# Layer three of a positional-bias network: tiles of four keys by thirty-two sums, or of eight keys by sixteen

## The chip, the cores and the metric

The kernel runs on one core of one Trainium2 chip. Such a core has five engines that each work through a queue of their own, in order: TensorE (matrix products; PE in the profile, PEld its weight loads), VectorE (DVE), ScalarE (ACT), GpSimd (POOL) and SyncE (SP, which here only starts transfers). They wait for one another through semaphores. Transfers are carried by sixteen DMA engines, whoever starts them. The metric is device time in microseconds for one execution; lower is better.

## The reference, cut to what matters

The reference is a transformer block with sampled keys, followed by a second attention layer. The part that the change touches is a small network that gives each pair of query and key an additive bias before the softmax:

```python
pos  = grid_q[:, :, None, :] - grid_kv[:, None, :, :]      # 16 groups, 1024 queries, 64 keys, 2
bias = sign(pos) * log1p(abs(pos))
bias = relu(bias @ cpb_w1 + cpb_b1)                         # 2 -> 128
bias = relu(bias @ cpb_w2 + cpb_b2)                         # 128 -> 128
bias = (bias @ cpb_w3 + cpb_b3)                             # 128 -> 1
sim  = einsum('bhid,bhjd->bhij', qh, kh) + bias
attn = softmax(sim, axis=-1)
```

There are 16 groups (2 images, 8 heads), so the network runs on 16 x 1024 x 64 pairs, all in float32. Its second layer is by far the largest product of the whole program.

## The kernel before

**Slots.** A group's 64 keys are cut into 16 slots of four keys; there are 256 slots, numbered `s` in the main loop (NG x NSL). One transfer for every four slots brings a table `fb` of the positional terms, from which ScalarE makes `ta` and `tb` for sixteen keys (`st_tables`).

**Layer 1** (`st_layer1`, L593) is one VectorE instruction per slot: it adds the two tables with broadcasts, clamps at zero and writes `h1`, 128 channels by 4096 (32 rows, 4 keys, 32 columns). Three buffers of `h1` let it run two slots ahead.

**Layer 2** (`st_layer2`, L610) is TensorE's. The 128 output channels are cut into four blocks `z` of 32. For one block, eight matmuls (two halves `h` of the queries, four keys `q`) write a PSUM tile of 128 partitions by 2 x 512: partition 32q + l holds lane l of key q. Each float32 matmul shows as two instructions in the profile. ScalarE empties the four tiles with bias and relu (L616 for `rx`, L618 for `ua` and `ub`).

**Adding the blocks.** The third layer is a weighted sum over the 128 channels. The size of each weight is applied early: even blocks are multiplied by a ratio of weights when VectorE adds them to their odd neighbour (`st_sum`, L626: `ua` from blocks 0 and 1, `ub` from blocks 2 and 3); only a sign per lane is left for the end. For that, the four channels that share a lane have been put in a fitting order by selections on GpSimd at the start (`swap`, L191 to L211). Then a transfer that adds at its destination, started by GpSimd (L628), puts `ub` onto `ua`. What is left of a slot is one tile `ua` of four keys by 32 sums.

**Layer 3** (`st_layer3`, L649) multiplies `ua` by `w3s`, a matrix of signs, to add the 32 lanes of each key. It runs once for every two slots, three slots after the first of them: four matmuls (two halves `h`, two slots `e`), each 32 output rows by 512. The rows of a group's 16 slots collect in one PSUM tile `sim`, which also takes the product of queries and keys (L640) at the group's end. The last two slots skip the adding transfer and use more matmuls instead.

**Order.** Within an engine, instructions run in the order in which a scheduler places them at build time, mostly that of the program; `tc.issue_after` pins single ones. On VectorE, a slot in the steady state is h of two slots ahead, then `ub` of the slot before, then `ua` of this slot. Background work (attention's sampling for later groups until about 1300 us, softmax steps for finished groups) is put between the slots on all engines. After the loop, at 1990 us, come an output projection (L822), an MLP (L875) and the second attention (L994, L1092), which the change doesn't touch.

Of the kernel before, what the change touches and what calls it, by code (L numbers as in the profile page):

```python
# [10 lines left out]
ALU = mybir.AluOpType  # L11
# [10 lines left out]
KT = 16  # L22
LAST = 2
KS = 6
# [12 lines left out]
    ("bq", 4), ("bv", 4), ("bp", 4), ("dwb", 1), ("cb1", 1), ("cb3", 1),  # L37
    ("w1x", 1), ("w1y", 1), ("cb2", 4), ("w3", 4), ("dww", 36),
]
# [8 lines left out]
@with_exitstack  # L48
def conv_seq_kernel(ctx: ExitStack, tc: tile.TileContext, x, xt, kst, cst, vec, wsm, outw, w1, w2, wl, out):
    nc = tc.nc  # L50


    cp = ctx.enter_context(tc.tile_pool(name="cp", bufs=1))
    kp = cp.tile([P, 384], F32, name="kp")
    vs = cp.tile([P, NV], F32, name="vs")
    nc.scalar.dma_start(out=vs, in_=vec)
    xv = x.rearrange("b (k p) n -> p k b n", p=P)
    ident = kp[:, 0:128]

# [9 lines left out]
    sc = cp.tile([P, 9], F32, name="sc")  # L69
    w3s = cp.tile([P, 60], F32, name="w3s")  # L70
    nc.gpsimd.memset(w3s, 0.0)

# [66 lines left out]
    with tc.tile_pool(name="lp", bufs=2) as lp:  # L139
# [29 lines left out]
        nc.scalar.dma_start(out=cs, in_=cst)  # L169
        nc.scalar.dma_start(out=kp, in_=kst)  # L170

# [17 lines left out]

        def swap(w, of, n):  # L190
            w = w.rearrange("p (z c) -> p z c", z=4)  # L191
            t = ph.tile([P, 10, n], F32, tag="hx" if n > 1 else "swap", name=f"swap{n}")
            g, ne, a1, a3, keep, t0, t1 = t[:, 0:4], t[:, 4], t[:, 5], t[:, 6], t[:, 7], t[:, 8], t[:, 9]
            nc.gpsimd.tensor_scalar(g, w, 0.0, None, ALU.is_ge)
            for o, u, v in ((ne, g[:, 1], g[:, 3]), (a1, g[:, 0], g[:, 1])):
                nc.gpsimd.tensor_tensor(o, u, v, ALU.subtract)
                nc.gpsimd.tensor_tensor(o, o, o, ALU.mult)
            nc.gpsimd.tensor_tensor(a1, a1, ne, ALU.mult)
            nc.gpsimd.tensor_tensor(a3, ne, a1, ALU.subtract)
            nc.gpsimd.tensor_scalar(keep, ne, -1.0, 1.0, ALU.mult, ALU.add)  # L200
            for dst, src in of:
                d, v = (e.rearrange("p (z c) -> p z c", z=4) for e in (dst, src))
                nc.gpsimd.tensor_copy(d[:, 2], v[:, 2])
                nc.gpsimd.tensor_tensor(d[:, 0], v[:, 0], keep, ALU.mult)
                for z, a in ((1, a1), (3, a3)):
                    nc.gpsimd.tensor_tensor(t0, v[:, z], a, ALU.mult)
                    nc.gpsimd.tensor_tensor(d[:, 0], d[:, 0], t0, ALU.add)
                    nc.gpsimd.tensor_scalar(t1, a, -1.0, 1.0, ALU.mult, ALU.add)
                    nc.gpsimd.tensor_tensor(t1, t1, v[:, z], ALU.mult)
                    nc.gpsimd.tensor_tensor(t0, v[:, 0], a, ALU.mult)  # L210
                    nc.gpsimd.tensor_tensor(d[:, z], t0, t1, ALU.add)  # L211

        swap(kp[:, 256:384], [(cw2, kp[:, 128:256])], 32)
        w3 = vs[:, VOFF["w3"] : VOFF["w3"] + 4]
        swap(w3, [(sc[:, 0:4], w3), (sc[:, 4:8], vs[:, VOFF["cb2"] : VOFF["cb2"] + 4])], 1)
        nc.gpsimd.tensor_scalar(sc[:, 8:9], sc[:, 1:2], 0.0, 2.0, ALU.is_ge, ALU.mult)
        nc.gpsimd.tensor_scalar(sc[:, 8:9], sc[:, 8:9], 1.0, None, ALU.subtract)
        nc.gpsimd.tensor_scalar(sc[:, 0:4], sc[:, 0:4], sc[:, 8:9], None, ALU.mult)
        for z in (1, 3):
            nc.gpsimd.tensor_tensor(sc[:, 4 + z : 5 + z], sc[:, 4 + z : 5 + z], sc[:, z : z + 1], ALU.mult)  # L220
        for u in range(4):
            nc.gpsimd.tensor_copy(w3s[32 * u : 32 * u + 32, 28 + u : 29 + u], sc[32 * u : 32 * u + 32, 8:9])
        state = {}
# [153 lines left out]
        def sample(ci):  # L377
# [23 lines left out]
            for i, (b, k) in enumerate(G):  # L401
# [29 lines left out]
                for f in range(2):  # L431
                    r = slice(64 * f, 64 * f + 64)
                    d = kvz[r, f, :].rearrange("p (e i t) -> p e i t", e=2, t=4)
                    v, u = (
                        t[r].rearrange("p (i e t) -> p e i t", e=2, t=4)
                        for t in (ps[:, 0:J], sg[:, 4, f, i * J : (i + 1) * J])
                    )
                    for e in range(2):
                        nc.vector.scalar_tensor_tensor(
                            d[:, e], v[:, e], bns[r, k : k + 1], u[:, e], ALU.mult, ALU.add  # L440
                        )
# [103 lines left out]
        for _ in head:  # L545
            pass
        next(v)
        next(n)
# [5 lines left out]
        NS = NG * NSL  # L554
        tabs, h1s, sums, sims, logits = {}, {}, {}, {}, {}
        evicted, raw = {}, {}
# [46 lines left out]
        def st_layer2(s):  # L603
            h1 = h1s.pop(s)
            r = []
            for z in range(4):
                ps = zp.tile([P, 2, 512], F32, name="ps2")
                for h in range(2):
                    for q in range(4):
                        nc.tensor.matmul(  # L610
                            ps[32 * q : 32 * q + 32, h, :], cw2[:, 32 * z : 32 * z + 32],
                            h1[:, 16 * h : 16 * h + 16, q, :], start=True, stop=True,
                        )
                o = lp.tile([P, 2, 512], F32, name=("rx", "ua", "rx", "ub")[z], bufs=(3, 5, 3, 4)[z])
                if z % 2 == 0:
                    nc.scalar.activation(o, ps, AF.Relu, bias=sc[:, 4 + z : 5 + z])  # L616
                else:
                    nc.scalar.activation(o, ps, AF.Relu, bias=sc[:, 4 + z : 5 + z], scale=sc[:, z : z + 1])  # L618
                r.append(o)
                if z % 2 == 1:  # L620
                    evicted.setdefault(s, []).append(nc.cur_bb.bb.instructions[-1])
            sums[s] = r

        def st_sum(s, z):
            r = [t.rearrange("p h n -> p (h n)") for t in sums[s][z : z + 2]]
            nc.vector.scalar_tensor_tensor(r[1], r[0], sc[:, z : z + 1], r[1], ALU.mult, ALU.add)  # L626
            if z == 2 and s < NS - LAST:
                nc.gpsimd.dma_start(out=sums[s][1], in_=sums[s][3], accum_op=ALU.add)  # L628

        def st_layer3(s):  # L630
            gi, i = divmod(s // 2, NSL // 2)
            b, k, f = groups[gi]
            if i == 0:
                sims[gi] = simp.tile([P, 512], F32, name="sim")
            if i == NSL // 2 - 1:
                assert state[chain_of[b, k][0]] is None
                for h in range(2):
                    for e in range(2):
# [4 lines left out]
                        )  # L643
            parts = (1,) if s < NS - LAST else (1, 3)
            for z in parts:
                for h in range(2):
                    for e in range(2):
                        q = 64 * h + 32 * e
                        nc.tensor.matmul(  # L649
                            sims[gi][q : q + 32, :], w3s[:, 28 - 4 * i : 60 - 4 * i], sums[s + e][z][:, h, :],  # L650
                            start=(i == 0), stop=(i == NSL // 2 - 1 and z == parts[-1]),
                        )
            for e in range(2):
                sums.pop(s + e)

# [62 lines left out]
        for s in range(NS):  # L718
            if s > 0:
                st_sum(s - 1, 2)  # L720
            if s % 4 == 0 and s // 4 + 1 < 4 * NG:
                load_tables(s // 4 + 1)
# [29 lines left out]
            if tail is not None:  # L752
                with tc.issue_after(evicted[s][s % 4 == 0]):
                    tail = tail if next(tail, 0) is None else None
            if s % 2 == 1 and s >= 3:
                st_layer3(s - 3)
                if (s - 2) % NSL == NSL - 1:
                    tail = softmax_steps(s // NSL - 1)
        st_sum(NS - 1, 2)
        st_layer3(NS - 2)  # L760
        tail = softmax_steps(NG - 1)
# [417 lines left out]


def _layout(np, inputs):
    a = {k: np.asarray(v) for k, v in inputs.items()}
# [6 lines left out]
    def twice(v):  # L1189
# [7 lines left out]
        "dwb": twice(L0["off_dw_b"].reshape(DH, 1)), "cb1": L0["cpb_b1"].reshape(P, 1),  # L1197
        "cb2": np.tile(L0["cpb_b2"].reshape(4, 32).T, (4, 1)),
        "w3": np.tile(L0["cpb_w3"].reshape(4, 32).T, (4, 1)),
        "cb3": np.broadcast_to(L0["cpb_b3"].reshape(1, 1), (P, 1)),  # L1200
# [26 lines left out]
    def quarters(w):  # L1227
# [8 lines left out]
        "xt": a["x"].reshape(B, NCH, P, 8, P).transpose(4, 0, 1, 3, 2),  # L1236
        "kst": np.concatenate(
            [np.eye(P, dtype=np.float32), L0["cpb_w2"], np.broadcast_to(L0["cpb_w3"].reshape(1, P), (P, P))],
            axis=1,
        ),  # L1240
        "cst": _constants(np), "vec": vec, "wsm": wsm,
# [25 lines left out]
```

## Time and profile before

| | us |
| --- | --- |
| Median of 3 runs (2735.78 to 2737.64) | 2737.45 |
| Span of the profiled execution | 2735.9 |
| First matmul of layer 2 | 41.70 |
| End of the slot loop (first projection matmul) | 1990.13 |
| Pair of slots in a quiet stretch (1423.88 to 1438.47) | 14.59 |
| h, one per slot on VectorE | 4.40 each |
| A sum of two blocks on VectorE | 1.28 each |
| Issue of an adding transfer on GpSimd | 0.87 each |

A profile page gives for each engine the busy time and its share of the span, then the span in 40 slices with the busy share of each in tenths, then the DMA queues, then the chain of work that ended last, followed back from the end. Under it stand groups of equal instructions: line, engine, operation, tile written and tiles read, shape and count, busy time and mean of one in ns, and behind the second bar how long the engine was idle just before them and what ended it. Lines on transfers give the size of one and the median time from issue to landing. Answers in order of time give start and length in us.

### The profile page before, as it was taken

To read this page: it belongs to the slowest core of one execution; us is meant where nothing else is said; L and a number is where in the kernel's file an instruction comes from. 1 tells how busy PE (TensorE), PEld (TensorE's weight loads), DVE (VectorE), ACT (ScalarE), POOL (GpSimd) and SP (SyncE) were. 2 spreads that over 40 slices of the span, in tenths; PEclk is the share of its full clock that TensorE was granted. 3 is DMA by queue.
4 is the path that set the end of the run, shared out by engine and by line. 5 is a ranking of instruction groups with operands and counts; after the bars stand their busy time and mean duration, and the time that the engine had idled before them with its cause. 6 is when DMAs were issued, how large, how long until landed. Compare 5 with 4: busy or idle time off the path is not lost.

```text
span 2735.9 us, 46606 instructions
## 1 busy us (share of the span) xinstructions
PE 2718.1 (99%) x20114; PEld 983.6 (36%) x20114; DVE 2242.0 (82%) x1331; ACT 1686.5 (62%) x2164; POOL 362.8 (13%) x426
## 2 busy tenths in 40 slices
PE   9999999999999999999999999999999999999999
PEld 3332323232334333334333333333344444446455
DVE  6999999998999899999999999999864574366454
ACT  4786897788878788876876776686722021124040
POOL 3111111111111111111111111111133333000000
PEclk9999999999999999999999999999999999999999
DMA  5444444444444443444444444444331011000000
GB/s 186 92 95 91 92 100 86 87 102 100 86 87 101 101 86 82 98 93 86 86 93 90 86 90 92 86 91 92 74 139 46 32 45 46 16 16 0 31 0 31
DMA packets 64685, 214.32 MB, mean 78 GB/s; under 512 B 11104, under 2 KB 13664, under 8 KB 61792
## 3 DMA queue, kind: packets, MB, share of 16 engines
q0 software_dynamic: 36864, 135.28, 26.7%
q1 hardware_dynamic: 26752, 74.98, 7.8%
q8 instruction: 159, 2.61, 0.4%
q10 hardware_dynamic: 864, 1.07, 0.1%
q14 instruction: 46, 0.38, 0.0%
HBM read 71.59 MB, written 6.55 MB: 29 GB/s over the span
## 4 chain that ended last, share of the span: by engine, by line
PE 92%; DVE 4%; ACT 2%; issue 1%; DMA 1%; SPq 0%; DVEq 0%; ACTq 0%
PE ps L610 59%; PE sw L875 14%; PE sw L994 9%; PE sim L649 4%; PE sw L1092 2%; DVE h L593 2%; PE sw L822 1%; PE psg L499 1%; PE sim L640 0%; DVE ua L626 0%; DVE ub L626 0%; DMA fb<-fdr 0%; PE pkv L425 0%; DVE xs L830 0%; ACT rx L616 0%
## 5 line engine op out<-in xcount | busy, mean ns | idle before, releaser
L610 PE MATMUL ps<-h,cw 128*32 128x512 f32 x16384 | 1791.2, 593 | 7.4 <-ACT rx L616 5.0
L593 DVE CUSTOM_DVE_ANT_1 h<-ta,tb 128x4096 f32<-128x4096 f32 (+1 forms) x257 | 1131.8, 4404 | 85.1 <-PE ps L610 81.5
L610 PEld LDWEIGHTS ps<-h,cw 128*32 128x32 f32 x16384 | 544.1, 110 | 1215.6 <-issue 1160.9
L616 ACT ACTIVATE rx<-ps,sc 128x1024 f32<-128x1024 f32 x512 | 568.4, 1110 | 219.8 <-PE ps L610 216.6
L628 POOL DMA_DIRECT2D ua<-ub x254 | 220.0, 866 | 1697.7 <-DVE ub L626 1609.9
L618 ACT ACTIVATE ua<-ps,sc 128x1024 f32<-128x1024 f32 x256 | 308.0, 1203 | 117.1 <-PE ps L610 116.8
L618 ACT ACTIVATE ub<-ps,sc 128x1024 f32<-128x1024 f32 x256 | 307.6, 1202 | 89.2 <-PE ps L610 88.9
L626 DVE SCALAR_TENSOR_TENSOR ua<-rx,sc,ua 128x1024 f32<-128x1024 f32 x256 | 327.3, 1278 | 32.6 <-ACT ua L618 32.6
L626 DVE SCALAR_TENSOR_TENSOR ub<-rx,sc,ub 128x1024 f32<-128x1024 f32 x256 | 326.8, 1276 | 5.8 <-ACT ub L618 5.6
L875 PE MATMUL sw<-xb,w1t 128*128 128x512 f32 x448 | 193.7, 592 | 1.3 <-DVE xs L121 1.3
L875 PE MATMUL sw<-hm,w2t 128*128 128x512 f32 x448 | 193.6, 592 | 0.0
L121 DVE TENSOR_TENSOR hm<-hm,sw 128x1024 f32<-128x1024 f32 x56 | 67.6, 1220 | 112.5 <-PE sw L875 112.3
L649 PE MATMUL sim<-ua,w3s 128*32 128x512 f32 x1024 | 135.7, 594 | 0.0
L875 PEld LDWEIGHTS sw<-xb,w1t 128*128 128x128 f32 x448 | 85.1, 190 | 108.8 <-issue 105.4
L875 PEld LDWEIGHTS sw<-hm,w2t 128*128 128x128 f32 x448 | 85.2, 190 | 107.1 <-issue 106.1
L884 ACT ACTIVATE hm<-hm,vs 128x512 f32<-128x512 f32 x64 | 42.7, 713 | 129.5 <-DVE hm L121 129.5
L121 DVE TENSOR_TENSOR xs<-xs,sw 128x1024 f32<-128x1024 f32 (+1 forms) x48 | 55.6, 1171 | 74.6 <-PE sw L994 36.0
L574 ACT ACTIVATE ta<-fb,vs 128x512 f32<-128x512 f32 x64 | 88.8, 1388 | 17.7 <-DMA fb<-fdr 17.7
L994 PE MATMUL sw<-aT,vt 128*128 128x512 f32 x224 | 96.7, 593 | 0.3 <-ACT aT L1074 0.3
L909 ACT COPY hm<-sw 128x1024 f32<-128x1024 f32 x8 | 8.1, 1009 | 132.4 <-PE sw L875 132.4
L103 POOL TENSOR_TENSOR w1t<-w1t 128x512 f32<-128x512 f32 x32 | 58.4, 1844 | 112.0 <-DMA w1t<-in_w 111.4
L290 ACT ACTIVATE prod<-qa,vs 128x56 f32<-128x56 f32 (+4 forms) x180 | 64.1, 442 | 0.0
(227 smaller groups left out, 1533.3 us busy)
## 6 DMA issues: line engine op xcount, KB each, us to landing
ua<-ub POOLq DMA_DIRECT2D x254, 512.0 KB, 4.6
fb<-fdr SPq DMA_DIRECT2D x64, 512.0 KB, 4.7
w1t<-in_w SPq DMA_DIRECT2D x8, 1024.0 KB, 4.9
w2t<-in_w SPq DMA_DIRECT2D x8, 1024.0 KB, 4.9
xn<-in_x SPq DMA_DIRECT2D x8, 512.0 KB, 5.1
xnt<-in_xt SPq DMA_DIRECT2D x8, 512.0 KB, 5.7
xs<-in_x SPq DMA_DIRECT2D x16, 256.0 KB, 5.7
out<-xs SPq DMA_DIRECT2D x16, 256.0 KB, 2.1
```

Of the source, the lines that this page charges most:

```text
L121: nc.vector.tensor_tensor(out, a, b_, op)
L290: nc.scalar.activation(dst, src, AF.Copy, scale=col("dww", 12 * m + t))
L574: nc.scalar.activation(ta.rearrange("p j x -> p x j"), fb[:, 0], AF.Identity, bias=col("cb1"), scale=col("w1x"))
L593: nc.vector._custom_dve(TENSOR_ADD_SAT, out=h1[:, y : y + step].rearrange("p y t x -> p (y t x)"), in0=a.unsqueeze(1).to_broadcast([P, ste ...
L610: nc.tensor.matmul(ps[32 * q : 32 * q + 32, h, :], cw2[:, 32 * z : 32 * z + 32], h1[:, 16 * h : 16 * h + 16, q, :], start=True, stop=True,)
L616: nc.scalar.activation(o, ps, AF.Relu, bias=sc[:, 4 + z : 5 + z])
L618: nc.scalar.activation(o, ps, AF.Relu, bias=sc[:, 4 + z : 5 + z], scale=sc[:, z : z + 1])
L626: nc.vector.scalar_tensor_tensor(r[1], r[0], sc[:, z : z + 1], r[1], ALU.mult, ALU.add)
L628: nc.gpsimd.dma_start(out=sums[s][1], in_=sums[s][3], accum_op=ALU.add)
L649: nc.tensor.matmul(sims[gi][q : q + 32, :], w3s[:, 28 - 4 * i : 60 - 4 * i], sums[s + e][z][:, h, :], start=(i == 0), stop=(i == NSL // 2 ...
L875: nc.tensor.matmul(ps[:, m, :], w[:, a, k, m * P : (m + 1) * P], x[:, b_, k, :], start=(k == 0), stop=(k == 1),)
L994: nc.tensor.matmul(ps[:, m, :], w[:, a, k, c + m * P : c + (m + 1) * P], x[b_][:, k, :], start=(k == 0), stop=(k == nk - 1),)
```

## The change

Two tiles of four keys by 32 sums become one of eight keys by 16 sums before layer 3 reads them. Channels are ordered by the sign of their third-layer weight, so that two neighbouring lanes (2l and 2l + 1) may be added before the sign is applied. `st_fold` adds the odd lanes of an even slot's tile onto its even lanes, `st_join` brings the odd lanes of the next slot into the freed odd lanes and adds that slot's even lanes to them. All three act on 64 of 128 partitions, every second one. The aim is to let layer 3 run once for four slots with the four matmuls that it used for two.

```diff
+        def lanes(s, i):
+            return sums[s][1].rearrange("(l e) h n -> l e (h n)", e=2)[:, i]
+        def st_fold(s):
+            with tc.issue_after(added[0]):
+                nc.gpsimd.dma_start(out=lanes(s, 0), in_=lanes(s, 1), accum_op=ALU.add)
+        def st_join(s):
+            nc.sync.dma_start(out=lanes(s, 1), in_=lanes(s + 1, 1))
+            with tc.issue_after(added[0]):
+                nc.gpsimd.dma_start(out=lanes(s, 1), in_=lanes(s + 1, 0), accum_op=ALU.add)
...
         def st_sum(s, z):
-            if z == 2 and s < NS - LAST:
+            if z == 2 and s < NS - 1:
                 nc.gpsimd.dma_start(out=sums[s][1], in_=sums[s][3], accum_op=ALU.add)
+                added[0] = nc.cur_bb.bb.instructions[-1]
...
         def st_layer3(s):
-            gi, i = divmod(s // 2, NSL // 2)
+            gi, i = divmod(s // 4, NSL // 4)
...
         for s in range(NS):
             if s > 0:
                 st_sum(s - 1, 2)
+            if s % 2 == 0 and 2 <= s < NS - 2:
+                st_fold(s - 2)
+            if s % 2 == 1 and 3 <= s < NS - 1:
+                st_join(s - 3)
...
-            if s % 2 == 1 and s >= 3:
-                st_layer3(s - 3)
+            if s % 4 == 2 and s >= 6:
+                st_layer3(s - 6)
```

`added[0]` is the newest adding transfer of a whole slot, so fold and join stand behind the next slot's in GpSimd's queue. The last four slots are not joined; they use other signs (`w3u`) and ten matmuls.

The sums get other buffers, twelve tiles as before:

```diff
-                o = lp.tile([P, 2, 512], F32, name=("rx", "ua", "rx", "ub")[z], bufs=(3, 5, 3, 4)[z])
+                name, bufs = (("rx", 3), (("ua", 4), ("uo", 2))[s % 2], ("rx", 3), ("ub", 3))[z]
+                o = lp.tile([P, 2, 512], F32, name=name, bufs=bufs)
```

At the start, the selections on GpSimd go, and an order of channels is computed instead: a load `pst` (transposed second-layer weights and index tables), two rank matmuls with one column each ahead of the query product, a dozen small operations, and later a matmul with a permutation and sixteen tiny ones, which give layer 2's weights and the scalars in the new order.

```diff
-        swap(kp[:, 256:384], [(cw2, kp[:, 128:256])], 32)
-        w3 = vs[:, VOFF["w3"] : VOFF["w3"] + 4]
-        swap(w3, [(sc[:, 0:4], w3), (sc[:, 4:8], vs[:, VOFF["cb2"] : VOFF["cb2"] + 4])], 1)
+        nc.tensor.matmul(ps[:, 0:1], tri, po_, start=True, stop=True)
+        nc.tensor.matmul(ps[:, 512:513], one, po_, start=True, stop=True)
...
+        def arrange():
+            ps = flat("perm")
+            nc.tensor.matmul(ps[:, 0:P], w2t, perm, start=True, stop=True)
+            for z in range(4):
+                for u in range(4):
+                    nc.tensor.matmul(
+                        ps[32 * u : 32 * u + 32, 512 + 2 * z : 514 + 2 * z], perm[:, 32 * z : 32 * z + 32], wb,
+                        start=True, stop=True,
+                    )
+            nc.scalar.copy(cw2, ps[:, 0:P])
...
         for _ in head:
             pass
+        arrange()
         next(v)
```

## The prediction

> **What bounds the kernel now.** I read the engines' busy times first, then the slices, the chain of waits, the groups, and last the stage in question by stretches and in order of time.
>
> ```profile
> PE 2718.1 (99%) x20114; PEld 983.6 (36%) x20114; DVE 2242.0 (82%) x1331; ACT 1686.5 (62%) x2164; POOL 362.8 (13%) x426
> PE   9999999999999999999999999999999999999999
> DVE  6999999998999899999999999999864574366454
> PE 92%; DVE 4%; ACT 2%; issue 1%; DMA 1%; SPq 0%; DVEq 0%; ACTq 0%
> L610 PE MATMUL ps<-h,cw 128*32 128x512 f32 x16384 | 1791.2, 593 | 7.4 <-ACT rx L616 5.0
> L649 PE MATMUL sim<-ua,w3s 128*32 128x512 f32 x1024 | 135.7, 594 | 0.0
> q0 software_dynamic: 36864, 135.28, 26.7%
> ua<-ub POOLq DMA_DIRECT2D x254, 512.0 KB, 4.6
> out<-xs SPq DMA_DIRECT2D x16, 256.0 KB, 2.1
> ```
>
> TensorE is busy 99% of the span and carries 92% of the chain: removed matmul time is real time unless something else takes over. That something is VectorE: in slices 2 to 28 (the slot loop, 43 to 1990 us) it stands at 9 nearly throughout. Layer 3 (L649) shows 135.7 us, but records overlap their neighbours, so I price it from the order of time, in a stretch without background work:
>
> ```profile
> 1423.88 13.92 PE L610 MATMUL ps<-h,cw 128*32 128x512 f32 x128
> 1430.99 4.42 DVE L593 CUSTOM_DVE_ANT_1 h<-ta,tb 128x4096 f32<-128x4096 f32 x1 [0.91 <-PE ps L610]
> 1436.91 0.87 POOL L628 DMA_DIRECT2D ua<-ub  x1 [6.84 <-DVE ub L626]
> 1437.61 1.04 PE L649 MATMUL sim<-ua,w3s 128*32 128x512 f32 x8
> 1438.47 13.92 PE L610 MATMUL ps<-h,cw 128*32 128x512 f32 x128
> ```
>
> From 1423.88 to 1438.47 two slots take 14.59 us. L610's 128 instructions run from 1423.88 to 1437.61 (13.73 us, 0.107 us each, a slot 6.87); L649's eight take the other 0.86 us, also 0.107 each. VectorE has 0.91 us idle here; back to back its slot is 6.73 us (starts of h at 1002.08, 1008.81, 1015.54). Where attention's other work runs on it as well, it has none:
>
> ```profile
> 1050.00:1100.00 50.00, 50.00 (x470) 15.75 (x466) 49.93 (x36) 42.00 (x63) 6.47 (x7) 1.00 0.39 80
> 1400.00:1450.00 50.00, 50.00 (x472) 15.10 (x464) 45.45 (x21) 34.44 (x32) 5.18 (x6) 1.00 0.47 96
> ```
>
> The columns after the length are PE, PEld, DVE, ACT and POOL busy us, clock, DMA share, GB/s. Both windows have a full TensorE; VectorE has 0.07 us left in one, 4.55 us in the other.
>
> [...] The trace disagrees for the adding transfers: 4.6 us to landing, and 26.7% of 2735.9 us over 254 of them is 2.87 us on the engines. [...] the trace has 2.1 us for out<-xs, to memory. [...] each link added below costs a full landing; before has no such link. [...] the issue of L628 takes 0.85 to 0.91 us beside h (L593), but 1.32 us where the small TENSOR_SCALAR of L383 falls on it. More issues on GpSimd should not slow VectorE.
>
> **The change part by part.**
> Removed: layer 3 runs once for four slots on eight-key tiles, not once for two. In the built order 516 matmuls become 262, so 254 fewer, two instructions each: 508 x 0.107 = **54.4 us** off TensorE, 0.86 per four slots, 1.4 per 50 us of loop.
> What VectorE lets through: its work is unchanged, so in each 50 us window the gain is at most its idle time. From 50 to 1300 us, 15 of 25 windows leave it at least 1.4 us (21 us in all); the other ten, at 48.74 to 50.00 busy, leave 4.0 us together. From 1300 to 1990 us every window has 2.7 us or more idle: 13.8 x 1.4 = 19.4. Sum 44.4; **10 us are lost to VectorE**.
> Added transfers: per pair of slots one fold (64 partitions, 256 KB), one plain copy on SP (256 KB), one join (256 KB): 126 of each. Issue: 252 more on GpSimd at 0.45 to 0.87 us, at most 219 us over 1947 us beside 220 us now; that engine mostly waits (1610 us for ub's sum). Engines: q0 goes from 26.7% to about 40% (252 x 1.44 us more). Neither binds.
> Their latency is the new wait. From the start T of a slot, sum ub ends and L628 issues at T+6.1 (1430.75 to 1436.91 above). The engines have it done at about +9.9 (landing less 0.8 of tail); the fold behind it needs half of 2.87: +11.3, landed +12.1. Copy on SP, 2.4 us[...]: +14.6. The join stands behind the next slot's L628 on GpSimd (issue at +13.0, engines done at +16.8): +1.4 +0.8 = landed **+19.1**. Layer 3 reads it three slots after T: 3 x 6.87 = **+20.6**. So 1.5 us to spare, against 3.0 before (L628 issued at +6.1 landed at +10.7 and was read two slots after T, at +13.7). Behind a late layer 3 stands all of layer 2 in TensorE's queue. A VectorE burst (the TENSOR_REDUCE of L305 is 2.98 us) puts the chain up to 1.5 us late if it falls in the half of the slots that feed a join: about one such per window in the 15 windows with room, 0.7 us each: **-10 us**. From 1300 us on, bursts are 1.3 us and fit.
> Bounds of the chain: if stride-2 halves take the engines the full 2.87 us and the copy 5.7 us (the slowest 256 KB load), landing is 13.5, 19.3, 23.9: 3.3 us late, each time. If only the copy is slow, 17.9 and 21.0: 0.4 late. If only the halves are, 20.5: just in time.
> Buffers: ua 4, uo 2, ub 3 for ua 5, ub 4. ub's is free when L628 has landed, a slot ahead of its reuse; uo's after the join, about 5 us ahead; ua's after layer 3, two slots ahead. Nothing.
> Start: layer 2's weights are now ordered on the chip. The first rank matmul stands ahead of psq in TensorE's queue and waits for a load that takes kp's place (issued at 4.56, 4.9 to landing: 9.5). psq goes from 7.1 to 9.85: +2.75 on both chains behind it (the taps on VectorE, psg on TensorE). Sixteen tiny matmuls and the permuting one then stand ahead of psu; at 0.07 to 0.115 us an instruction (put, L523: 1.84 us for 16) that is 2.3 to 3.9 us, middle 2.7. TensorE's chain ends at 41.7 before its first slot, so both count: **+5.4** (3 to 7). The removed GpSimd selections ran beside this and give nothing.
> End: last layer 3 has four more instructions (0.4) and needs slot 254's landed sum: **+1**.
> Sum: 54.4 - 10 - 10 - 5.4 - 1 = 28, so 2737.5 - 28 = **2709 us**.
>
> **The rivals.**
> A, as worked out: 2709. For it: the windows' idle times. Chance 0.50.
> B, TensorE alone decides: VectorE's full windows are only its backlog catching up, and the chain is never late: 54.4 - 6.4 = 48, 2689. For it: TensorE is full in those windows too, so nobody starved. Against: 150 us in a row (1000 to 1150) at 49.9 is no backlog. Chance 0.15.
> C, VectorE takes all of the first part: nothing gained up to 1300 us, 19.4 - 6.4 = 13, 2724. For it: the shorter reserve of 1.5 us couples TensorE to every burst. Against: 15 windows with 1.4 us or more. Chance 0.18.
> D, the late transfer takes the place of the matmul: slower. With the chain 1.5 us late at the 63 layer-3 steps that read joins: +94 - 54.4 + 6.4 = +46, 2783; at the upper bound (3.3 late, 208 us) 2897. For it: three landings in a row in front of an engine with an in-order queue, and the reserve is smaller than my error on one landing. Against: both short legs hide behind the next slot's L628, so one slow link alone costs at most 0.4. Chance 0.17.
>
> **How the numbers follow.** The forecast is A's 2709. The range runs from B's 2689 to 2742: it holds A, C, most of B and mild forms of D, and leaves out the rest of D (0.15) and what of B lies below 2689 (0.05). Faster by over 0.2% (under 2732): A, B and most of C, 0.79. Within 0.2%: the bad end of C and the mild end of D, 0.05. Slower: 0.16.
>
> **What would show it.** Layer 3 with half its instructions and a loop end near 1960 us instead of 1990. VectorE at 49 or more in most windows up to 1300. The first slot's matmuls near 47 us instead of 42. Landings: fold about 5 us after its issue, copy 2 to 3, join 3 to 4.5. Waits of layer 3 for a DMA, short and before 1300 us; if they appear in every group of four slots, D is right; if there are none and VectorE sits at 49, C or A with a smaller stall. VectorE's h longer than 4.42 us would mean that transfers or descriptors do slow it, which I have priced at nothing.

## The result and the profile after

The kernel after the change takes **2782.25 us** (median of 4 runs, 2778.10 to 2787.11) against 2737.2 us before: ratio 1.0166, 95% interval 1.0149 to 1.0184. It is 45 us slower, where 28 us less was forecast. The profiled execution of after is the slowest of the four (2787.1).

These lines of the page of the kernel after answer to the ones shown of before: busy time, slices, the queue of the transfers that GpSimd starts, chain, and the groups of layer 2, of layer 3 and of the two new adding transfers.

```profile
PE 2707.1 (97%) x19644; PEld 1210.8 (43%) x19644; DVE 2247.6 (81%) x1337; ACT 1682.3 (60%) x2167; POOL 575.5 (21%) x625
PE   9998999999999999999998999999999999999999
q0 software_dynamic: 57168, 201.88, 38.3%
PE 89%; ACT 5%; issue 4%; DVE 1%; DMA 1%; SPq 0%; ACTq 0%; POOL 0%; DVEq 0%
L633 PE MATMUL ps<-h,cw 128*32 128x512 f32 x16384 | 1827.0, 595 | 16.4 <-ACT rx L640 15.4
L664 POOL DMA_DIRECT2D ua<-ua x126 | 154.9, 1230 | 1.1 <-issue 1.1
L669 POOL DMA_DIRECT2D ua<-uo x126 | 109.2, 866 | 458.8 <-DMA ua<-uo 439.5
L698 PE MATMUL sim<-ua,w3f 128*32 128x512 f32 x504 | 111.7, 606 | 50.5 <-issue 50.5
```

Layer 3 has half its matmuls (504 on joined tiles for 1024) and, as a group, 24 us less busy time. But it had no idle time ahead of it before, and now has 50.5 us. The chain gives "issue" 4% where it was 1%: time in which the view finds no releaser. The table of waits of before and of after names the same instructions on the weight load's side; the columns are what waited, what it was put down to, us in total, times, longest.

```profile
PEld sim L649 <- issue: 72.7, 238, 0.8
```

```profile
PEld sim L698 <- issue: 112.1, 135, 5.4
PE sim L698 <- issue: 50.5, 29, 4.5
```

Before has many short waits of the weight loads, none over 0.8 us, and no idle time of layer 3's matmuls (0.0 on its page). One of 5.4 us is something else, and "issue" doesn't say what. Only the order of time with the landings does. Of each four slots, two pairs are folded and joined; here are the first and the second pair of one four (start, then the landing in us from issue). Layer 3 needs both at the same time, so the first pair has two slots more to spare:

| | first pair, no table load | second pair, with one |
| --- | --- | --- |
| adding transfer `uo<-ub` (L652) | 1441.04, landed after 4.9 | 1457.14, 7.5 |
| table load `fb<-fdr` (L587) | none | 1457.61, 4.9 |
| fold (L664) | 1441.62, 5.6 | 1457.72, 8.2 |
| adding transfer of the next slot `ua<-ub` (L652) | 1447.90, 4.6 | 1464.01, 6.7 |
| copy (L667) | 1447.39, 2.2 | 1466.03, 5.2 |
| join (L669) | 1450.16, 3.8 | 1471.73, 3.3 |
| layer 3 goes on | no wait of its own | 1475.08 |

The second pair in order of time (start, length, and in brackets the idle time before it):

```profile
1457.14 0.90 POOL L652 DMA_DIRECT2D uo<-ub  x1 [6.13 <-DVE ub L650]
1457.61 0.33 SPq L587 DMA_DIRECT2D fb<-fdr  x1
1457.72 1.20 POOL L664 DMA_DIRECT2D ua<-ua  x1
...
1471.27 0.59 PE L698 MATMUL sim<-ua,w3f 128*32 128x512 f32 x1
1471.73 0.85 POOL L669 DMA_DIRECT2D ua<-uo  x1 [6.83 <-DMA ua<-uo]
...
1475.08 0.18 PEld L698 LDWEIGHTS sim<-ua,w3f 128*32 128x32 f32 x6 [4.12 <-issue]
1475.11 0.63 PE L698 MATMUL sim<-ua,w3f 128*32 128x512 f32 x3 [3.25 <-issue]
```

The reader is to see three things. The table load, 512 KB, is started on SP 0.1 us ahead of the fold and 0.47 us after the adding transfer. The join of the second pair is issued 0.46 us after layer 3's second instruction has begun. Layer 3 goes on when that join has landed (1471.73 + 3.3), and layer 2 stands behind it.

It is always the same pair: a table load comes once in four slots, when ScalarE has read the old table, and that is when the fold of the second pair of the four is at work, the one with the least time before layer 3. At 59 of the 63 steps with joins the load starts within 4 us of the second pair's fold, at none within 4 us of the first's; the folds land in 8.0 and 6.2 us at the median. Layer 3 stood idle for over 0.3 us at 27 of its 63 steps with joins, 50.0 us in all, spread over the whole loop (22.5 us before 1300 us, 27.5 after). Meeting the load is not enough for a stall: at the median layer 3 began 14.0 us after the issue of `uo<-ub` at these 27 steps and the join landed 17.0 us after it, and 15.6 and 15.9 at the other 36, most of which met a load too.

The stalls cost more than their length. After the one at 1471 to 1475 the clock column (the third from the end of each row) falls to half:

```profile
1474.00:1476.00 2.00, 0.89 (x10) 0.53 (x14) 2.00 (x1) 0.00 (x0) 0.38 (x1) 1.00 0.98 180
1476.00:1478.00 2.00, 2.00 (x16) 1.13 (x12) 1.44 (x2) 0.00 (x0) 0.26 (x1) 0.51 1.09 207
1478.00:1480.00 2.00, 2.00 (x17) 0.94 (x13) 0.00 (x0) 0.37 (x1) 0.64 (x1) 0.64 0.72 137
1480.00:1482.00 2.00, 2.00 (x26) 1.03 (x20) 0.00 (x0) 1.40 (x2) 0.00 (x0) 1.00 0.98 203
```

TensorE is "busy" 2.00 us in each of the last three, but only 16, 17 and then 26 of its instructions fall into them.

### The profile page after: what moved, and what is told of

Its sections match the earlier page's. It is cut to its first block, busy times and chain, and to the rows that moved or that the text cites. A ratio compares the mean times of both kernels' runs of the same rounds, so it can differ in the third digit from the quotient of the medians.

```text
span 2785.3 us, 47016 instructions
## 1 busy us (share of the span) xinstructions
PE 2707.1 (97%) x19644; PEld 1210.8 (43%) x19644; DVE 2247.6 (81%) x1337; ACT 1682.3 (60%) x2167; POOL 575.5 (21%) x625
## 3 DMA queue, kind: packets, MB, share of 16 engines
q0 software_dynamic: 57168, 201.88, 38.3%
## 4 chain that ended last, share of the span: by engine, by line
PE 89%; ACT 5%; issue 4%; DVE 1%; DMA 1%; SPq 0%; ACTq 0%; POOL 0%; DVEq 0%
PE ps L633 57%; PE sw L928 14%; PE sw L1047 9%; PE sim L698 3%; PE sw L1145 2%; ACT rx L640 1%; PE psg L521 1%; PE sw L875 1%; ACT prod L312 1%; ACT ub L642 1%; PE sim L682 0%; ACT sx L745 0%; DVE h L616 0%; DMA fb<-fdr 0%; PE pkv L447 0%
## 5 line engine op out<-in xcount | busy, mean ns | idle before, releaser
L633 PE MATMUL ps<-h,cw 128*32 128x512 f32 x16384 | 1827.0, 595 | 16.4 <-ACT rx L640 15.4
L633 PEld LDWEIGHTS ps<-h,cw 128*32 128x32 f32 x16384 | 780.3, 110 | 998.3 <-issue 867.0
L616 DVE CUSTOM_DVE_ANT_1 h<-ta,tb 128x4096 f32<-128x4096 f32 (+1 forms) x257 | 1131.8, 4404 | 63.4 <-PE ps L633 58.5
L652 POOL DMA_DIRECT2D ua<-ub x128 | 114.8, 897 | 679.1 <-DVE ub L650 642.2
L650 DVE SCALAR_TENSOR_TENSOR uo<-rx,sc,uo 128x1024 f32<-128x1024 f32 x128 | 164.0, 1281 | 83.9 <-ACT uo L642 83.8
L669 POOL DMA_DIRECT2D ua<-uo x126 | 109.2, 866 | 458.8 <-DMA ua<-uo 439.5
L652 POOL DMA_DIRECT2D uo<-ub x127 | 118.9, 936 | 396.1 <-DVE ub L650 353.4
L642 ACT ACTIVATE uo<-ps,sc 128x1024 f32<-128x1024 f32 x128 | 154.3, 1206 | 56.1 <-PE ps L633 56.1
L642 ACT ACTIVATE ua<-ps,sc 128x1024 f32<-128x1024 f32 x128 | 154.2, 1205 | 51.4 <-PE ps L633 50.8
L650 DVE SCALAR_TENSOR_TENSOR ua<-rx,sc,ua 128x1024 f32<-128x1024 f32 x128 | 163.7, 1279 | 8.2 <-ACT ua L642 8.2
L698 PE MATMUL sim<-ua,w3f 128*32 128x512 f32 x504 | 111.7, 606 | 50.5 <-issue 50.5
L664 POOL DMA_DIRECT2D ua<-ua x126 | 154.9, 1230 | 1.1 <-issue 1.1
```

The costliest lines, as they stand in the source:

```text
L616: nc.vector._custom_dve(TENSOR_ADD_SAT, out=h1[:, y : y + step].rearrange("p y t x -> p (y t x)"), in0=a.unsqueeze(1).to_broadcast([P, ste ...
L633: nc.tensor.matmul(ps[32 * q : 32 * q + 32, h, :], cw2[:, 32 * z : 32 * z + 32], h1[:, 16 * h : 16 * h + 16, q, :], start=True, stop=True,)
L664: nc.gpsimd.dma_start(out=lanes(s, 0), in_=lanes(s, 1), accum_op=ALU.add)
L669: nc.gpsimd.dma_start(out=lanes(s, 1), in_=lanes(s + 1, 0), accum_op=ALU.add)
L698: nc.tensor.matmul(sims[gi][q : q + 32, :], w_, t[:, h, :], start=(i == 0), stop=(i == NSL // 4 - 1 and m == len(parts[e]) - 1),)
```

## The experiments

Each was timed against the kernel before on the same chip; the first four shared one chip, the last four another. My theory: **the joined sum lands too late for layer 3, because the fold shares the DMA engines with the table load**. Rivals: GpSimd's or the DMA engines' load as such; VectorE slowed or made the bound; the new start.

| Run | us | ratio to before (95%) |
| --- | --- | --- |
| after | 2782.25 | 1.0166 (1.0149 to 1.0184) |
| e1_l3_late: layer 3 one slot later | 2703.05 | 0.9877 (0.9862 to 0.9892) |
| e2_no_moves: no fold, no join | 2702.52 | 0.9876 (0.9861 to 0.9891) |
| e3_fb_once: no table loads | 2715.47 | 0.9923 (0.9908 to 0.9938) |
| e4_fold_first: fold ahead of the next slot's transfer | 2755.51 | 1.0075 (1.0058 to 1.0092) |
| e5_fb_move: table load behind the join | 2723.06 | 0.9955 (0.9939 to 0.9972) |
| e6_before_relief: before, one sum less | 2737.78 | 1.0001 (0.9992 to 1.0010) |
| e7_l3_late_relief: e1, one sum less | 2696.85 | 0.9855 (0.9840 to 0.9869) |
| e8_l3_late_start: e1, rank work behind psq and psg | 2697.39 | 0.9856 (0.9841 to 0.9870) |

**e1_l3_late.** Nothing is left out or moved but layer 3, which runs a slot later.

```diff
-            if s % 4 == 2 and s >= 6:
-                st_layer3(s - 6)
-                if (s - 2) % NSL == 0:
+            if s % 4 == 3 and s >= 7:
+                st_layer3(s - 7)
+                if (s - 3) % NSL == 0:
```

> Layer 3 is run one slot later (at s % 4 == 3, reading slots s - 7 to s - 4), all else as in the changed kernel. Theory 1, the chain of three landings (fold, copy, join) is late at layer 3 and TensorE's queue stands still behind it: 6.9 us more time covers lateness of up to 4 us, layer 3's waits for 'issue' fall from 112 us to under 50, the clock stays at 1.00, 2700 to 2712 us. Rival, VectorE is what holds TensorE up and layer 3 only shows it: no more than 15 us off the changed kernel's 2782.

Measured 2703.05 us, 79 us under after. All transfers are still there with similar landings: fold 6.6 us, copy 2.3, join 3.9 (6.8, 3.1 and 3.5 in after). What is gone is the long wait; its row in the table of waits of this run:

```profile
PEld sim L698 <- issue: 39.6, 129, 0.8
```

So the lateness alone makes the change a loss. The load on GpSimd and on the DMA engines as such is out: it is the same here (q0 40.1%).

**e2_no_moves.** Fold and join are left out, so layer 3 reads sums that lack lanes; its matmuls are those of after.

```diff
             if s > 0:
                 st_sum(s - 1, 2)
-            if s % 2 == 0 and 2 <= s < NS - 2:
-                st_fold(s - 2)
-            if s % 2 == 1 and 3 <= s < NS - 1:
-                st_join(s - 3)
```

> Leaves out fold and join and so half of the sums; layer 3 still runs once for four slots with half the matmuls, start and order of channels as in the changed kernel. It prices the matmul saving alone. If VectorE's idle time lets 44 of 54.4 us through and the start costs 5.4: 2737 - 44 + 6.4 = 2699. If TensorE alone decides: 2689. If VectorE takes all of the first 1300 us: 2724. If VectorE, not the transfers, made the changed kernel slow: over 2750.

Measured 2702.52 us, and 2703.05 with all the transfers and a slot more of time (e1). 378 transfers, 252 of them issued by GpSimd, and 14 points of q0's share (40.1% there, 26.3% here) are thus worth 0.5 us together, within what these runs can tell from nothing. VectorE isn't slowed by them: h takes 4404 ns in the mean in after, with all of them, as in before.

**e3_fb_once.** Table loads after the first two are left out; all later slots use the second one's table.

```diff
             assert ci in state
+            if c > 1:
+                raw[c] = only[0]
+                return
             fb = lp.tile([P, 2, W, KT], F32, name="fb", bufs=1)
```

> Leaves out all table loads fb but the first two (all later slots use the second one's table); fold, copy, join and layer 3 as in the changed kernel. Theory 1a, the load of fb always meets the fold that layer 3 waits for (7.9 to 8.2 us to landing beside a load, 5.6 to 6.2 without): folds land at 6 throughout, copies at 2.3 to 3.5, most waits of layer 3 go, 2700 to 2735 us. Theory 1b, three landings in a row are too long by themselves: stays above 2760.

Measured 2715.47 us. The transfer lines of this run's page and its waits:

```profile
uo<-ub POOLq DMA_DIRECT2D x127, 512.0 KB, 4.6
ua<-ua POOLq DMA_DIRECT2D x126, 256.0 KB, 5.5
ua<-uo SPq DMA_DIRECT2D x126, 256.0 KB, 2.3
ua<-uo POOLq DMA_DIRECT2D x126, 256.0 KB, 4.1
```

```profile
PEld sim L702 <- issue: 55.5, 128, 4.5
```

In after, the first three lines read 5.5, 6.8 and 3.1. 67 of the 79 us between after and e1 go with the table loads. Not all of the 67 need be the meeting with the fold: without loads ScalarE doesn't wait for tables either (19.6 us in three waits of `ta` in after), and layer 2's waits for ScalarE (rows `PE ps <- ACT rx`) fall from 15.4 to 7.1 us. The other 12.4 us are mostly seven stalls of layer 3, 10.7 us together. In the one that ends at 1287.76, VectorE runs back to back (h starts at 1266.07, 1272.80 and 1279.53, 6.73 apart) and lags: `uo<-ub` is issued at 1271.98, only 12.3 us before layer 3's first matmul, where TensorE's pace would give 14.5.

**e5_fb_move.** The same table load, left in, but started by GpSimd behind the join of a four's second pair, the one that layer 3 waits for.

```diff
-            nc.sync.dma_start(
+            queue.dma_start(
...
+            if s % 4 == 1 and s // 4 + 2 < 4 * NG and chain_of[groups[(s // 4 + 2) // 4][:2]][0] in state:
+                with tc.issue_after(added[1] if s > 1 else added[0]):
+                    load_tables(s // 4 + 2, nc.gpsimd)
```

> Nothing left out: the load of the table fb is started by GpSimd behind the join that layer 3 waits for, three slots before its table is needed, instead of by SP as soon as ScalarE has read the old one. Layer 3 stands where the changed kernel has it. If the meeting of that load with the fold is the cause (theory 1a), the folds that layer 3 waits for land in 5.5 to 6.5 us, and the time comes near that without the loads, 2715: 2710 to 2730. If the loads cost by their bytes, wherever they are: 2750 or more.

Measured 2723.06 us, 59 under after with every byte still moved. Its transfer lines:

```profile
uo<-ub POOLq DMA_DIRECT2D x127, 512.0 KB, 4.6
ua<-ua POOLq DMA_DIRECT2D x126, 256.0 KB, 5.8
ua<-uo SPq DMA_DIRECT2D x126, 256.0 KB, 2.3
ua<-uo POOLq DMA_DIRECT2D x126, 256.0 KB, 4.4
fb<-fdr POOLq DMA_DIRECT2D x60, 512.0 KB, 5.7
```

The fold lands a microsecond sooner and the copy 0.8, though q0 now stands at 43.7%. So the moment of the load is what hurts, not the amount moved. The edit also takes the load off SP, which starts the copies; but in after the copy is issued 0.1 us after the fold's landing (1457.72 + 8.2 and 1466.03 above), so SP's queue did not hold the chain up. Six stalls of layer 3 are left, 6.0 us together. In the 7.6 us to e3, timed on the other chip, layer 2's waits for ScalarE are the larger part by the traces (16.7 us against 7.1), and layer 3's stalls go the other way (6.0 against 10.7).

**e4_fold_first.** The fold stands ahead of the next slot's adding transfer.

```diff
-            if s > 0:
-                st_sum(s - 1, 2)
             if s % 2 == 0 and 2 <= s < NS - 2:
                 st_fold(s - 2)
+            if s > 0:
+                st_sum(s - 1, 2)
```

> The fold is put ahead of the next slot's adding transfer in GpSimd's queue, not behind it. The fold needs only its own slot's sum, which landed half a slot earlier, so it can start about 3 us sooner and doesn't queue on the engines behind 512 KB. Theory 1: 3 us sooner at each layer 3 takes most of the lateness of 1.5 to 4 us: 2710 to 2745. If what counts is the load of fb, which still meets it: under 20 us gained, over 2760.

Measured 2755.51 us (2746.18 to 2759.98), between the bands of both theories, so neither was right. The fold's landing falls from 6.8 to 3.7 us, but `uo<-ub` takes 6.1, and the copy needs that one too. The waits now name the last link:

```profile
PEld sim L698 <- DMA ua<-uo: 46.4, 32, 4.9
PE sim L698 <- DMA ua<-uo: 23.9, 18, 4.0
```

This trace is of the fastest of the four runs. Half of layer 3's idle time is left in it (23.9 for 50.5). The order is worth 27 us, and does not cure the lateness: with the fold ahead, `uo<-ub` is what lands late.

**e6_before_relief and e7_l3_late_relief.** These ask for what of the 54.4 us never came. Both leave out the sum of blocks 0 and 1 (1.28 us a slot on VectorE); e6 does so in the kernel before, e7 in e1.

```diff
-            st_sum(s, 0)
             if bg is not None:
```

> The kernel before, leaving out the sum of blocks 0 and 1 (one of the two VectorE sums of each slot, 1.28 us of 6.73). TensorE was full, so little changes: 2725 to 2737 us. It is the base for the next run.

> The kernel with layer 3 one slot later, leaving out the same sum. If VectorE's full windows held back 13 of the 54.4 us there (theory A of the prediction), they don't now: 48 us (54.4 less the 5.8 of the start) under the kernel before with the same sum left out, about 2680 to 2689. If the missing 13 us are TensorE's own (joins of layer 3 with layer 2 in its queue, clock): 34 us under it, as with the sums in.

e6: 2737.78 us, no change. With VectorE at 71%, before is as fast as with 82%: VectorE does not bind it. e7: 2696.85, 40.9 under e6, halfway between the 34 and the 48 that the two theories gave: e1 is 33 under the before of its chip, so e7 is 7 to 8 us better off than e1. Not all of that is the sum that was left out. The first slot matmul of e7's trace is at 45.3 us and that of e1's at 47.5, a difference that is there before the first sum runs (see "Start" below). By the slot loops alone, from the first slot matmul to the first of the projection, e7 takes 1904.3 us and e6 1949.1, so 44.8 of the 54.4 us arrive; e1 takes 1907.0 and before 1948.4, so 41.4 arrive. VectorE thus holds about 3 us by the loops, 7 to 8 at most. The rest is not VectorE's. TensorE's idle time in the loop is 13.9 us in e7 and 8.9 in e6, 16.9 in e1 and 7.4 in before, and the largest row of the waits, in this order, is

```profile
PE ps L633 <- ACT rx L640: 13.3, 13, 3.7
```

```profile
PE ps L610 <- ACT rx L616: 8.5, 4, 6.0
```

```profile
PE ps L633 <- ACT rx L640: 10.2, 15, 1.9
```

```profile
PE ps L610 <- ACT rx L616: 5.0, 4, 2.7
```

Layer 2 waits for ScalarE to empty its PSUM. What makes ScalarE late was not tried.

**e8_l3_late_start.** e1, with the rank matmuls and their arithmetic behind psq and psg, in `sim`'s PSUM.

```diff
-        ps = flat("rank")
...
+        def rank():
+            ps = simp.tile([P, 512], F32, name="sim")
...
+        with tc.issue_after(newest(mybir.EngineType.PE)):
+            rank()
         marks.append(newest(mybir.EngineType.PE))
```

> Layer 3 one slot later, and the rank matmuls with what follows them are put behind the query product psq and the first weight products psg (in PSUM of sim), not ahead of them. psq starts at 7.1 us again, without TensorE's 3 us of idle time and half clock behind it; left are the permuting matmul and sixteen tiny ones, 0.8 us. First matmul of layer 2 at 42.5 to 43.5 instead of 47.5: 4 to 5 us under 2703, 2698 to 2700. If the start is set by the other chain (taps, tables) whose end was at 43.4 before, the same.

Measured 2697.39 us, 39.6 under the before of its chip where e1 is 33.3 under that of its own; the first slot matmul of its trace in order of time:

```profile
42.59 5.79 PE L636 MATMUL ps<-h,cw 128*32 128x512 f32 x52
```

That is 4.9 us sooner than in e1 (47.5) and 0.9 later than before (41.7). The traces with the start of after have it between 45.3 and 48.3, so by the traces the edit is worth 2.7 to 5.7 us. This version beats both kernels: 40 us under before, 85 under after, with the whole computation in it.

## Why the prediction was wrong

**The step that failed is the latency sum.** It put the chain at T + 19.1 against a need at T + 20.6, with "1.5 us to spare". Its terms were sized without the table load, as if only the chain's own transfers and the next adding transfer used the DMA engines. That each link costs a full landing is what the stalled pair shows: the copy is issued 0.1 us after the fold's landing, the join 0.5 us after the copy's.
- Fold landed at T + 12.1. Measured in the stalled pair above (T, the slot's first layer-2 instruction, is at 1450.59): issue of `uo<-ub` at T + 6.6 (forecast 6.1), 0.6 to the fold's issue, 8.2 to landing, so T + 15.3. In the pair without a table load, T + 12.7: the arithmetic was near for an empty queue. Half the engines' time for half a tile and the tail of 0.8 us were the author's estimates: the half held ("Small terms"), and in before no bytes of the transfer issued at 1436.91 move after 1440.8, 0.6 us ahead of its landing.
- Copy 2.4 us. Without the load 2.2; in the stalled pair 5.2, median over all 3.1. The load itself had landed by then (1462.5): the late fold had pushed the copy behind the next slot's adding transfer (1464.01). So T + 20.6. (The 2.4 us was the author's estimate, above the 2.1 us that before shows for `out<-xs`, also started by SP.)
- The join, which the prediction let stand behind the next slot's adding transfer, was hidden there only as long as the copy landed ahead of that transfer. With the copy at T + 20.6 its full 3.3 us and 0.5 to its issue came on top: T + 24.4. In the pair without the load it landed at T + 19.4.

The table load stood in the kernel, once in four slots, and the prediction worked without it. "q0 goes from 26.7% to about 40%. Neither binds" was right as a share (38.3%) and no answer to the question: an average over the span doesn't say what runs at the microsecond in which a chain with 1.5 us to spare needs the DMA engines. Of the bounds, two moved one link at a time (slow copy alone 0.4 late, slow halves alone just in time); in the stalled pair three landings grew together (7.5 us for 4.9, 8.2 for 5.6, 5.2 for 2.2). (The 5.7 us for a slow copy is the slowest 256 KB load of the page; the full list of before has two more, of 8.4 and 9.1.) The third, all links slow, 3.3 us late, came near the stalled pair, but from halves that are slow by themselves. Transfers that different engines start did get in each other's way: beside the load on SP, GpSimd's adding transfer took 7.5 us for 4.9. In windows of 1 us the DMA share is 0.99 to 1.06 from 1442 to 1446 without the load, and 0.87 to 1.06 from 1459 to 1464 with it.

**Rival D named the mechanism, and was given 0.17.** Its 2783 is 1 us from what was measured, but not by its own terms. It had 63 steps 1.5 us late, 94 us. Against e1 the loop of the traces lost 87 us (1994.0 from 1907.0), from 27 idle waits: after a stall TensorE is behind and the next chain has more room (the 15.6 us for 14.0 above). That the sum met the measured time is luck. The 50 us of idle matmuls are not the whole: weight loads of layer 3 waited 112.1 us for 39.6 in e1, 72.5 more. For the 22 beyond the idle time there is only an estimate: in the stall shown above the weight load waited 4.12 us and the matmul 3.25, 0.87 less, and 27 times that is 23. And in 2 us windows the clock took 13.6 us for 1.7 in e1: 12 more (5.1 of the 13.6 after one stall of 6.68 us at 272, where ScalarE waits 8.4 us for a table load and layer 2 for ScalarE). Together 84 of the 87, as a tally of two traces.

**What TensorE saves.** 508 instructions at 0.107 us, 54.4: the loop of before took 1948.4 us (41.7 to 1990.1), that of e1 1907.0, so 41.4 arrived. So 13 were lost in e1, where the prediction had 10 for VectorE's full windows and 10 for bursts. In size both were near: e1, with room for bursts, lost 13, and e3, without, 12.4 more. In cause the first was mostly wrong: VectorE holds about 3 of the 13 by the loops, and 9.5 of them are idle time of TensorE (16.9 us for 7.4), most of it behind ScalarE. The second was sized by the longest reduction of L305, 2.98 us; in the trace of before only 3 of its 32 reach 2.9 us, the others at most 1.6. That these sizes came out near is in good part luck.

**Start.** First slot matmul at 46.5, forecast about 47, +4.8 for +5.4. The parts were not those of the sum. psq began at 9.90 (forecast 9.85), but took 1.98 us for 1.09, and psg's 24 matmuls 12.19 for 10.57 (TensorE had been idle for 3.02 us up to 8.99, and its granted clock was 0.50 to 0.57 from 8 to 14 us and 0.72 from 14 to 16, for 1.00 in before; e8, without the rank work there, starts at 42.6); the permuting matmul and the sixteen tiny ones took 0.38 and 0.43 us, not 2.7. Errors that cancel are no hit. Nor is the first matmul fixed to a microsecond: the traces with this start (after, e1 to e5, e7) have it at 45.3 to 48.3 us and psq's start at 9.5 to 11.3; why was not tried.

**End.** +1: from the loop's end to the span's end there are 745.8 us before and 744.8 after; nothing to be seen.

**Small terms.** VectorE's h, priced at no change, takes 4404 ns in the mean in both kernels, with 254 adding transfers issued by GpSimd and with 507. The join landed in 3.5 us (forecast 3 to 4.5), though fold and copy took 6.8 and 3.1 at the median (about 5, and 2 to 3). The fold's issue shows 1.20 us for 0.45 to 0.87 because it follows another issue (see the end), with no consequence that e2 shows. The DMA engines' time for a half transfer, an estimate of 1.44 us, held: e1's q0 of 40.1% less e2's 26.3%, over 252, is 1.48 us each.

**A's number.** With the lateness gone, e1's 2703.05 is 6 us under A's 2709 and between A and B: that part of the sum was worth having. What the forecast named as D's sign, waits of layer 3 for a DMA in every group, came in 27 of 63 groups and under the name of "issue".

**The range** ended at 2742, so it left D out. For a chain whose reserve is smaller than the error on one of its links, "late" had to be in it.

## What to carry to other kernels

Before you add links to a chain of transfers, list every transfer that can be in flight during it, on all queues, and size the landings with those beside it; an average share of the DMA engines answers another question. If the reserve is smaller than the error of one link, buy a stage of delay for the consumer: here one slot, in the buffers that were already there, turned 45 us lost into 33 gained. Ask for each wait you risk what stands behind it: here, with all of layer 2 behind and TensorE 99% busy, 50 us more idle time went with 87 us more of the loop.

## What the runs showed of the hardware

- The half clock after a short stall. In after, gaps of 2.01, 2.67, 2.90, 3.25 and 4.52 us between matmuls in front of layer 3 were each followed by a granted clock near 0.5, and each time 1.7 us were lost by it (in the windows above (1 - 0.51) x 2 + (1 - 0.64) x 2). Five other gaps of 2.24 to 2.90 us (ending at 102, 484, 795, 1135 and 1791) were not followed by it, so the length of the gap alone did not decide. e1, with no such gap in layer 3, has one drop in its loop, to 0.51, at a gap of 4.05 us.
- A 512 KB load stretches both transfers that it meets: `uo<-ub` 4.9 to 7.5 us, fold 5.6 to 8.2, while its own landing, 4.9, was near its median of 4.6. At the median of all steps of after, the first pairs have 5.1 and 6.2 us, the second pairs 7.3 and 8.0.
- GpSimd's issue of a transfer shows 0.85 to 0.90 us where it stands alone, and more where it starts before the one ahead of it has ended. The fold, 0.58 us behind `uo<-ub` in after, shows 1.20; in e4 it shows 0.85 alone (its median) and 1.19 behind a join, and `uo<-ub` behind both 1.54. In before, four of the 254 issues show 1.19 to 1.33, those on which the TENSOR_SCALAR of L383 falls. In e4:

```profile
1440.22 0.85 POOL L669 DMA_DIRECT2D ua<-uo  x1 [5.41 <-DMA ua<-uo]
1440.76 1.19 POOL L664 DMA_DIRECT2D ua<-ua  x1
1441.31 1.54 POOL L652 DMA_DIRECT2D uo<-ub  x1
...
1453.42 0.85 POOL L664 DMA_DIRECT2D ua<-ua  x1 [2.22 <-DMA ua<-ub]
```
